# Two halves of the TensorE array: issue order of the forward transform's column products and second-pole products

## The chip, the cores and the metric

The kernel runs on one NeuronCore of a Trainium2 chip, as one launch. The metric is the device time of that launch in microseconds. The engines of the core are written as in the profile: PE (TensorE, matrix products), PEld (its weight loads), DVE (VectorE), ACT (ScalarE), POOL (GpSimd) and SP (which issues DMAs). All data are 32-bit floats.

## The reference

The input x has shape 16 x 16 x 256 x 256 (batch, channel, rows, columns). Two layers follow one another, and each is a group norm (8 groups of two channels) with a block behind it and the input added at the end. Layer 0 is a Laplace neural operator; layer 1 is a pair of small convolutions with an involution and a channel gate. The change is in layer 0:

```python
alpha = jnp.fft.fft2(x, axes=(-2, -1))
A  = 1.0 / (omega1[:, None, None, None] - weights_pole1[None])
Bm = 1.0 / (omega2[:, None, None, None] - weights_pole2[None])
S = jnp.einsum('ikpq,oikp,xikq->oxik', weights_residue, A, Bm)
output_residue1 = jnp.einsum('biox,oxik->bkox', alpha, S)
C = jnp.einsum('biox,oikp->bikpx', alpha, A)
D = jnp.einsum('bikpx,xikq->bikpq', C, Bm)
output_residue2 = jnp.einsum('bikpq,ikpq->bkpq', D, weights_residue)
```

`fft2` is done as two rounds of matrix products (first along rows, then along columns), and the projections on the poles, `C` and `D`, are matrix products as well.

## The kernel before

`forward` calls four stages one after another: `layer0_forward` (forward transform and pole projections), `layer0_mix` (channel mixing in frequency), `layer0_back` (inverse transform and second group norm) and `layer1`. The change is inside `layer0_forward` alone.

**The 64 steps.** A step handles one batch element `b` and one group `cg` of four channels. In step i PE works, in this order:

- `gn_mean` (L34): the group mean for the next step, and in the middle of the rows `gn_var` (L42). Between the two DVE computes `gnq` (L36 to L39) from the mean, so `gn_var` waits for DVE.
- `rows` (called twice, for two channels each): per channel eight products of 128 x 128 by 128 columns, alternately `pu` (L207, the row transform) and `pv` (L214, the first poles). ACT copies half of `pu` (`right`, L222), DVE adds and subtracts the halves into the spectrum tile `u` (L224), and ACT scales `pv` into `vt` (L231).
- `poles` (L241): the second poles, `pd`, for four channels.
- `columns` (L313): the column transform of the batch element before, out of `u`. Each call takes up to four of the 33 groups of frequencies. Steps with `cg` 0, 1 and 2 make two calls; a step with `cg` 3 makes three, the last for the single 33rd group. ACT moves `px` to `o` (L320), and POOL starts the DMAs that store `o` (L329).

The first four steps have no `columns`; after the last step all nine calls for the last batch element stand back to back. From step 4 on, one piece of the generator `tables` (the tables for the later stages, mostly DVE work, L400 to L530, and 16 small matrix products, L437) is put in per step until it runs out. PE's order is the order of the code (`manual_schedule` for PE); the order of the other engines is made by the scheduler. In `columns` the accumulator `px` has two buffers, and `o` has two.

**Halves of the array.** A product whose stationary operand has only 64 columns occupies half of the 128 columns of the array. Its output lands in PSUM partitions 0 to 63 or 64 to 127, according to the half. In `poles`, `a` selects the half (`pd[64 * a : ...]`); in `columns`, `k` does (`ps[64 * k : ...]`). A product of 32-bit floats is two instructions in the trace, so each call of `matmul` makes two weight loads and two MATMUL records. A chain of four products for one half is therefore eight records.

A product of the same shape as that in `columns`, 128 x 64 by 256 columns, stands in the next stage (`residues`, L635), and there the half is the innermost loop.

Of the kernel before, what the change touches and what calls it, by code (L numbers as in the profile page):

```python
# [72 lines left out]
def layer0_forward(ctx, tc, d, al, bd, tabs):  # L73
# [160 lines left out]
    def poles(cg, vts, acc):  # L234

        pd = psd.tile([P, 2, P], F32, tag="pd", name="pd")
        for j, vt in enumerate(vts):
            for a in range(2):
                ch = 4 * cg + 2 * j + a
                for n, (xh, k) in enumerate(((0, 0), (0, 1), (1, 0), (1, 1))):  # L240
                    nc.tensor.matmul(  # L241
                        pd[64 * a : 64 * a + 64, j],
                        lhsT=vt[:, a, xh, 64 * k : 64 * k + 64],
                        rhs=bt[:, xh, ch, 1 - k : 3 - k].rearrange("p l m -> p (l m)"),
                        start=n == 0,
                        stop=n == 3,
                    )
        gs = slice(2 * cg, 2 * cg + 2)

        def times(out, part, coef):  # L250
            shape = [P, 2, part.shape[2] // M, M]
            nc.vector.tensor_tensor(
                out.rearrange("p g (k q) -> p g k q", q=M),
                part.rearrange("p g (k q) -> p g k q", q=M),
                coef[:, gs].unsqueeze(2).to_broadcast(shape),
                ALU.mult,
            )

        t = dp.tile([P, 2, P], F32, tag="t", name="t")
        first = acc if cg == 0 else dp.tile([P, 2, P], F32, tag="t1", name="t1")  # L260
        times(first, pd, cr)
        times(t[:, :, :64], pd[:, :, 64:], ci)
        times(t[:, :, 64:], pd[:, :, :64], ci)
        if cg:
            nc.gpsimd.tensor_tensor(acc, acc, first, ALU.add)
        nc.gpsimd.tensor_tensor(acc[:, :, :64], acc[:, :, :64], t[:, :, :64], ALU.subtract)
        nc.gpsimd.tensor_tensor(acc[:, :, 64:], acc[:, :, 64:], t[:, :, 64:], ALU.add)
# [34 lines left out]
    def columns(b, g0, rsc):  # L302

        u = us[b % 2]
        n = min(4, NF - g0)
        o = op.tile([P, 2, 2, N], F32, tag="o", name="o")
        for j in range(0, n, 2):
            lanes = 64 * min(2, n - j)
            ps = psx.tile([P, 2, 2, H], F32, tag="px", name="px")
            for k in range(min(2, n - j)):  # L310
                for h in range(2):
                    for part in range(2):
                        nc.tensor.matmul(  # L313
                            ps[64 * k : 64 * k + 64, :, h],
                            lhsT=u[:, h, part, g0 + j + k].rearrange("p f c -> p (f c)"),
                            rhs=wxn[:, h, part],
                            start=part == 0,
                            stop=part == 1,
                        )
            nc.scalar.activation(  # L320
                o[:lanes, j // 2],
                ps[:lanes].rearrange("p v h x -> p v (h x)"),
                AF.Copy,
                scale=rsc[:lanes],
            )
        for k in range(min(2, n)):
            w = (n - k + 1) // 2
            for v in range(2):
                nc.gpsimd.dma_start(  # L329
                    out=al[g0 + k : g0 + n : 2, v, :, b].rearrange("g p x -> p g x"),  # L330
                    in_=o[64 * k : 64 * k + 64, :w, v],
                )
# [3 lines left out]
    with tc.manual_schedule(engines={mybir.EngineType.PE}):  # L336
# [6 lines left out]
        for i, (b, cg) in enumerate(steps):  # L343
            now, following = ready, iter(())
            if i + 1 < len(steps):
                following = halves(*steps[i + 1], *fetched.pop(0))
                next(following)
            v0 = rows(b, cg, 0, *now)
            next(following, None)
            if b and cg == 0:  # L350
                rsc = finish(b - 1, acc)
            v1 = rows(b, cg, 1, *now)
            ready = next(following, None)
            if cg == 0:
                acc = dp.tile([P, 2, P], F32, tag="acc", name="acc")
            if i == 0:
                table("2", *table_inputs("2"))
                passing.close()
            poles(cg, (v0, v1), acc)
            if b:  # L360
                for g0 in range(8 * cg, 8 * cg + 8 if cg < 3 else NF, 4):
                    columns(b - 1, g0, rsc)
            if i + 2 < len(steps):
                fetched.append(fetch(*steps[i + 2]))
            if i >= 4:
                next(pieces, None)
# [3 lines left out]
        for g0 in range(0, NF, 4):  # L370
            columns(nb - 1, g0, rsc)
# [1061 lines left out]
```

## Time and profile before

| | |
|---|---|
| device time, median of 3 | 7627.89 us (7627.58 to 7629.81) |
| span of the profiled execution | 7634.0 us |
| PE busy | 7110.6 us, 93% |
| DVE busy | 4906.0 us, 64% |
| ACT busy | 3674.3 us, 48% |
| POOL busy | 2832.8 us, 37% |
| `layer0_forward` | about the first 1420 us of the span |

A row of the table of groups reads: source line, engine, operation, output and inputs, the size of the array that is used (128*64 is 128 rows by 64 columns), shape of the moving operand, number of records, then busy time in us and mean duration of one record in ns, then idle time before it and what ended that. Durations of matrix products overlap because they are pipelined: 385 ns is the duration of one record, and the busy time is that of the union of all.

### The profile page before, as it was taken

To read this page: it belongs to the slowest core of one execution; us is meant where nothing else is said; L and a number is where in the kernel's file an instruction comes from. 1 tells how busy PE (TensorE), PEld (TensorE's weight loads), DVE (VectorE), ACT (ScalarE), POOL (GpSimd) and SP (SyncE) were. 2 spreads that over 40 slices of the span, in tenths; PEclk is the share of its full clock that TensorE was granted. 3 is DMA by queue.
4 is the path that set the end of the run, shared out by engine and by line. 5 is a ranking of instruction groups with operands and counts; after the bars stand their busy time and mean duration, and the time that the engine had idled before them with its cause. 6 is when DMAs were issued, how large, how long until landed. Compare 5 with 4: busy or idle time off the path is not lost. (4 is left out here: it accounts for less than half of the span.)

```text
span 7634.0 us, 147451 instructions
## 1 busy us (share of the span) xinstructions
PE 7110.6 (93%) x58728; PEld 4078.3 (53%) x58728; DVE 4906.0 (64%) x9184; ACT 3674.3 (48%) x5387; POOL 2832.8 (37%) x3616
## 2 busy tenths in 40 slices
PE   7889999799999998999979999999999999999997
PEld 5778888566666666777723333333333333333332
DVE  8999875366666665666656666666666666666662
ACT  2223333366666663111146655665665666565662
POOL 2334444211111111111145545555545555545552
PEclk9999999899999999999989999999999999999998
DMA  3344444333333335877757888899888898888886
GB/s 97 113 116 125 113 119 109 113 96 95 97 95 100 97 98 161 259 245 248 232 151 219 233 241 249 244 267 258 247 246 248 245 267 259 251 242 246 246 267 204
DMA packets 936290, 1442.20 MB, mean 189 GB/s; under 512 B 91866, under 2 KB 807958, under 8 KB 903606
## 3 DMA queue, kind: packets, MB, share of 16 engines
q1 hardware_dynamic: 792374, 958.51, 44.5%
q0 software_dynamic: 143232, 474.25, 19.7%
q8 instruction: 469, 7.68, 0.4%
q14 instruction: 215, 1.76, 0.1%
HBM read 875.87 MB, written 556.47 MB: 188 GB/s over the span
## 5 line engine op out<-in xcount | busy, mean ns | idle before, releaser
L1021 ACT ACTIVATE wide<-c,b 32x512 f32<-32x512 f32 x2176 | 1479.5, 680 | 371.9 <-PE c L972 319.7
L1049 DVE TENSOR_TENSOR t<-pd,r 64x512 f32<-64x512 f32 x1088 | 744.1, 684 | 1324.0 <-PE pd L1041 1301.0
L1052 DVE TENSOR_TENSOR top<-pd,t 32x512 f32<-32x512 f32 x2176 | 1503.1, 691 | 54.2 <-DMA cf<-top 1.4
L1115 PE MATMUL c2ps<-rows,c 128*32 128x512 f32 x12288 | 1392.4, 600 | 22.5 <-ACT e L1124 13.8
L972 PE MATMUL c<-z,w 102*128 102x512 f32 x2048 | 1052.2, 645 | 140.5 <-ACT wide L1021 117.1
L1033 POOL COPY wide<-wide 32x1031 f32<-32x1031 f32 (+1 forms) x576 | 569.0, 988 | 1392.7 <-ACT wide L1021 1365.4
L1041 PE MATMUL pd<-wide,dw 128*128 128x512 f32 x2048 | 1014.2, 617 | 5.9 <-ACT r L1009 3.5
L1115 PEld LDWEIGHTS c2ps<-rows,c 128*32 128x32 f32 x12288 | 388.0, 109 | 994.0 <-issue 889.4
L972 PEld LDWEIGHTS c<-z,w 102*128 102x128 f32 x2048 | 398.7, 197 | 703.4 <-issue 514.1
L1041 PEld LDWEIGHTS pd<-wide,dw 128*128 128x128 f32 x2048 | 377.2, 194 | 626.7 <-issue 456.7
L709 POOL DMA_DIRECT2D hd<-h x254 | 188.6, 742 | 1281.9 <-DVE h L705 1262.0
L1124 ACT ACTIVATE e<-c2ps,b 128x512 f32<-128x512 f32 x256 | 176.0, 687 | 857.5 <-PE c2ps L1115 854.8
L1034 POOL COPY wide<-wide 32x1031 f32<-32x1031 f32 (+1 forms) x576 | 572.3, 994 | 35.8
L313 PE MATMUL px<-wxn,u 128*64 128x256 f32 x4224 | 558.9, 385 | 2.6 <-ACT o L320 2.3
L839 PE MATMUL py<-h,iy 128*128 128x256 f32 x2048 | 541.6, 383 | 5.2 <-issue 5.2
L635 PE MATMUL ps<-tt,lt 128*64 128x256 f32 x4224 | 497.0, 385 | 37.8 <-DVE lt L621 34.0
L692 PE MATMUL ph<-ix,yt 64*128 64x256 f32 x4128 | 503.5, 391 | 7.4 <-issue 6.8
L313 PEld LDWEIGHTS px<-wxn,u 128*64 128x64 f32 x4224 | 401.0, 136 | 128.2 <-ACT o L320 5.7
L692 PEld LDWEIGHTS ph<-ix,yt 64*128 64x128 f32 x4128 | 393.6, 190 | 93.9 <-issue 46.5
L839 PEld LDWEIGHTS py<-h,iy 128*128 128x128 f32 x2048 | 385.2, 191 | 108.4 <-issue 50.0
L207 PE MATMUL pu<-fy,eo 128*128 128x128 f32 x2048 | 424.7, 291 | 12.0 <-DVE u L224 8.3
L594 DVE TENSOR_SCALAR alb<-alc,m 128x1024 f32<-128x1024 f32 x330 | 418.9, 1394 | 0.0
(202 smaller groups left out, 10008.6 us busy)
## 6 DMA issues: line engine op xcount, KB each, us to landing
rows<-cf SPq DMA_DIRECT2D x128, 2176.0 KB
z<-zn SPq DMA_DIRECT2D x768, 256.0 KB
cf<-top POOLq DMA_DIRECT2D x512, 240.0 KB, 7.3
cf<-bot POOLq DMA_DIRECT2D x96, 840.0 KB, 10.7
alc<-al SPq DMA_DIRECT2D x264, 256.0 KB
zn<-zb SPq DMA_DIRECT2D x128, 516.0 KB
o<-zn SPq DMA_DIRECT2D x64, 1032.0 KB
z<-in_x SPq DMA_DIRECT2D x64, 1024.0 KB
```

What stands on the lines that cost most here:

```text
L313: nc.tensor.matmul(ps[64 * k : 64 * k + 64, :, h], lhsT=u[:, h, part, g0 + j + k].rearrange("p f c -> p (f c)"), rhs=wxn[:, h, part], star ...
L635: nc.tensor.matmul(ps[64 * h : 64 * h + 64, v], lhsT=lt[:, h, k, 1 - v : 3 - v].rearrange("p l f c -> p (l f c)"), rhs=tt[:, h, k], start= ...
L692: nc.tensor.matmul(ph[q][:, e], lhsT=yt[lanes, i].rearrange("p t k -> p (t k)"), rhs=ix[lanes, i], start=n == 0, stop=n == 3,)
L839: nc.tensor.matmul(py[:, yh], lhsT=iy[:, v, ys], rhs=h[:, k, v], start=v == 0, stop=False)
L972: nc.tensor.matmul(ps[:, q], lhsT=w, rhs=cols[:, 1 - q], start=True, stop=True)
L1021: nc.scalar.activation(self.feat[64 - 32 * q : 96 - 32 * q, f, self.groups[g], :H], ps[32 * f : 32 * f + 32, q], AF.Mish, bias=b1[0][32 * ...
L1033: nc.gpsimd.tensor_copy(flat[0:32, f, 1:m], flat[64:96, f, 0 : m - 1])
L1034: nc.gpsimd.tensor_copy(flat[96:128, f, 0 : m - 1], flat[32:64, f, 1:m])
L1041: nc.tensor.matmul(ps, lhsT=dwt if self.tail else dw, rhs=self.feat[:, f, cs, :H], start=True, stop=True,)
L1049: nc.vector.tensor_tensor(t[64:128], ps[:64], self.r[:, cs], ALU.mult)
L1052: nc.vector.tensor_tensor(self.top[32 * f : 32 * f + 32, cs, q], ps[lanes], t[lanes], ALU.add)
L1115: nc.tensor.matmul(ps[32 * j : 32 * j + 32], lhsT=c2[:, blk, dx, :], rhs=t[:, 4 * j + blk : 4 * j + blk + 4, x : x + H], start=(blk, dx) = ...
```

## The change

The loops over the half move inward. In `poles` the four products of a chain are now the outer loop and the half `a` the inner one, and in `columns` the half `k` goes inside `h` and `part`. The products, their operands, their accumulation per half and their number stay the same: 2112 products in `columns` and 1024 in `poles`. Consecutive products now go to different halves of the array, so that two of them can run side by side. Building both programs shows the same order of instructions on DVE, ACT, POOL and SP.

```diff
         for j, vt in enumerate(vts):
-            for a in range(2):
-                ch = 4 * cg + 2 * j + a
-                for n, (xh, k) in enumerate(((0, 0), (0, 1), (1, 0), (1, 1))):
+            for n, (xh, k) in enumerate(((0, 0), (0, 1), (1, 0), (1, 1))):
+                for a in range(2):
+                    ch = 4 * cg + 2 * j + a
                     nc.tensor.matmul(
                         pd[64 * a : 64 * a + 64, j],
...
             ps = psx.tile([P, 2, 2, H], F32, tag="px", name="px")
-            for k in range(min(2, n - j)):
-                for h in range(2):
-                    for part in range(2):
+            for h in range(2):
+                for part in range(2):
+                    for k in range(min(2, n - j)):
                         nc.tensor.matmul(
                             ps[64 * k : 64 * k + 64, :, h],
```

## The prediction

> **What bounds the kernel now.** I read the groups of PE first, then busy time by stage, then PE's timeline in one step, then who waits for whom. All edits are in `layer0_forward`, so only its stretch of the span matters. The groups show the row to be changed and a twin that already alternates the halves:
>
> ```profile
> L313 PE MATMUL px<-wxn,u 128*64 128x256 f32 x4224 | 558.9, 385 | 2.6 <-ACT o L320 2.3
> L635 PE MATMUL ps<-tt,lt 128*64 128x256 f32 x4224 | 497.0, 385 | 37.8 <-DVE lt L621 34.0 <-issue 3.8
> L241 PE MATMUL pd<-bt,v 128*64 128x128 f32 x2048 | 164.6, 279 | 0.0
> ```
>
> The first two have the same shape, the same 4224 records and the same 385 ns each, yet the union is 558.9 us against 497.0. So the gain to be had is of the order of 62 us, and not the half of 559. The timeline of one step and of one burst of the twin say why:
>
> ```profile
> 1019.62 2.24 PE L241 MATMUL pd<-bt,v 128*64 128x128 f32 x29
> 1021.59 0.43 PE L313 MATMUL px<-wxn,u 128*64 128x256 f32 x1
> 1021.70 0.38 PE L241 MATMUL pd<-bt,v 128*64 128x128 f32 x2
> 1021.86 0.38 PE L313 MATMUL px<-wxn,u 128*64 128x256 f32 x1
> 1021.91 0.27 PE L241 MATMUL pd<-bt,v 128*64 128x128 f32 x1
> 1022.08 7.90 PE L313 MATMUL px<-wxn,u 128*64 128x256 f32 x62
> 1029.90 0.38 PE L34 MATMUL gn_mean<-mv,ones 128*128 128x2 f32 x2
> ```
> ```profile
> 1607.23 3.67 PE L635 MATMUL ps<-tt,lt 128*64 128x256 f32 x32
> ```
>
> The first `px` starts at 1021.59, before the last three `pd`, although it stands behind them in the program: PE already lets the next chain, which is for the other half, start before the chain ahead has ended. Record by record, starts in the middle of `px` follow 216, 6, 210, 57, 159, 57, 159, 57 ns, again and again: eight records (one chain) in 920 ns, or 115 ns each. One half alone would need 8 x 216 = 1726. In the twin the starts go 209, 7, 209, 7: two records in 215.8 ns, 108 each. What order costs today is mainly at the ends of a run: the first chain goes half alone, and the last four records go alone at 216 each.
>
> Next, the stages of the forward transform (columns: length, then busy us and records of PE, PEld, DVE, ACT, POOL, then clock, DMA share, GB/s):
>
> ```profile
> 166.40:552.20 385.80, 336.81 (x2662) 294.14 (x2661) 354.45 (x1047) 105.00 (x194) 137.84 (x189) 0.92 0.40 114
> 552.20:1019.60 467.40, 456.20 (x4065) 391.96 (x4064) 426.07 (x1085) 178.49 (x311) 219.65 (x300) 1.00 0.44 119
> 1019.60:1369.10 349.50, 349.50 (x3194) 304.36 (x3193) 187.30 (x568) 107.45 (x213) 166.05 (x234) 1.00 0.40 107
> ```
>
> Three regimes: steps 5 to 19, with table pieces, where DVE is busy 92%; steps 20 to 43, where PE is at 98% and DVE at 91%; and steps 44 to 62, where PE is busy for all of 349.50 us. The waits agree. The first line below is PE's in 166 to 545 us, the others are DVE's in 552 to 1019 us:
>
> ```profile
> PE gn_var L42 <- DVE gnq L39: 45.1, 15, 6.0
> ```
> ```profile
> DVE gnq L36 <- PE gn_mean L34: 10.8, 9, 2.0
> DVE arg L525 <- ACT n L523: 8.4, 10, 1.6
> DVE arg L515 <- DMA ed<-arg: 8.0, 6, 2.2
> DVE st L174 <- DMA z<-in_x: 7.6, 6, 2.5
> DVE u L224 <- ACT right L222: 1.1, 3, 0.6
> ```
>
> In the first regime PE waits for DVE in every step. In the second DVE waits for PE only 12 us in all.
>
> **What the Trainium skill says.** "TensorE: Matmul & The Clock Gate", Part 3, says that products in different column groups run side by side; the twin's 108 ns per record, half of the 216 that a lone half shows, agrees. The same part calls the order of matmuls strictly first in, first out, with only weight loads pulled ahead. The trace contradicts that for two halves (the `px` at 1021.59), and I take the trace: it is why the gain is small. Its Part 1 says that PE falls to half clock after an idle window of some 3.4 us. In steps 6 to 19 some 15 to 29 of the 64 row records start at 210 ns or so in place of 112, each time behind a gap of 2.0 to 6.2 us between two starts, so shorter idles suffice here.
>
> **The change part by part.** Nothing is added or removed, and no other engine's order moves. Only starts on PE change.
>
> *poles, per step.* Now 32 records from 1019.62 to the first `px` at 1021.59: 1.97 us. Alternating, they are 16 pairs. The middle of the present run, where both halves work, shows a pair in 109 ns, and the first record shows its weight load as 160 in place of 109. So 0.160 + 15 x 0.109 = 1.80 us: 0.18 saved.
>
> *columns, a step with two calls (64 records).* From the first `px` to `gn_mean` now 1029.90 - 1021.59 = 8.31 us. Alternating: 32 pairs at the twin's 215.8 ns. The last pair starts 31 x 0.2158 = 6.69 us after the first, and `gn_mean` follows the last start by 0.309 as today: 7.00 us. Saved: 1.31. Together 1.49 us per step.
>
> *columns, a step with cg 3 (72 records).* The 33rd group has only one half. Today it costs 0.92 us more (the run is 9.47 against 8.55 us to the first row product), because it runs beside the chain ahead. With all pairs full, its eight records are alone: 8 x 0.2158 = 1.73. So 0.81 of the 1.49 goes back: 0.68 saved.
>
> *Sum by regime.* Steps 44 to 62 are 15 of the first kind and 4 of the second: 15 x 1.49 + 4 x 0.68 = 25.1 us, all on the path. No other engine stops it: a step of 18.07 us becomes 16.58, where DVE has some 10 us of work, POOL 8.7, ACT 5.3. The waits of DVE for the input z there are for a step three ahead.
>
> Steps 20 to 43 would save 18 x 1.49 + 6 x 0.68 = 30.9 on PE, which takes PE's own 443.5 us (18 steps of 18.07 and 6 of 19.70) to 412.6. Counting each step by itself, DVE is busy 420 us in them, so DVE becomes the bound. What can go is what DVE waits for PE: 10.8 + 1.1 = 12 us; and part of the 8.4 for ACT's sine, which stands behind `o` in ACT's order, and `o` waits for `px`. I take 15 us. The DMA waits stay.
>
> Steps 5 to 19: `gn_var` waits for DVE in each, 2.0 to 6.2 us. An earlier end of `columns` makes this wait longer by the same amount. I take 0; a longer idle could keep PE cold for a few records more (-3), and the waits of DVE for `right` could shrink (+8).
>
> Steps 0 to 4: about 2 us (step 4 is bound by PE, the first four have `poles` alone). After step 63, nine calls stand back to back, 264 records in 33.9 us, 4.1 us a call, already above PE's 3.68 because `o` waits for its stores (ACT `o` on DMA, up to 2.3 us); PE's faster 3.45 brings little. With step 63 itself, 2 us.
>
> Sum: 25.1 + 15 + 0 + 2 + 2 = 44 us. 7627.9 - 44 = 7584.
>
> **The rivals.** *Second regime gains next to nothing:* DVE keeps its pace and PE goes cold in the gaps that open. For it: idles of 0.8 to 2.2 us before `gn_var` already stand in steps 21, 24, 32, 36 and 40, and 1.5 more brings them to the length that turned the clock down earlier. Against it: DVE's wait for `gn_mean` is real. Then 25 + 3 + 2 + 2 = 32: 7596.
>
> *Everything on PE's side pays:* the second regime saves its 31 and the first 8. For it: PE is at 98% in the second. Against it: DVE's 420 us. Then 25 + 31 + 8 + 4 = 68: 7560.
>
> *No change:* PE's own look-ahead already overlaps all that can be overlapped. Against it: the twin's 62 us. 7628.
>
> *Slower:* if alternation left each weight load open, a pair would take 216 + 51 (the 430 ns of the first record of a chain against 379) = 267 ns, and in `poles` 160: 31 x 0.267 + 0.309 = 8.59 us, 0.28 more than the 8.31 of today, and 16 x 0.160 - 1.97 = 0.59 more, together 0.87 a step. Over the 43 steps from 20 on that is 37 us, less where DVE hides it, say 25: 7653. Against it: the twin shows 260 once per burst and then 209.
>
> **How the numbers follow.** The forecast (a gain of 36 to 55) gets 0.55, the poor second regime 0.22, all of PE's side 0.13, no change 0.06, slower 0.04. The first three are faster by over 15 us: 0.90. The range reaches from a little beyond the large gain, 7558, to a little beyond the poor one, 7606, which leaves out no change and slower (0.10) and a tail of the rest.
>
> **What would show it right or wrong.** Starts in L313 alternating 209 and 7; its union near 495 to 505; a step in the third regime of 16.6 us, 19.0 with cg 3; the second regime near 452 us with DVE the busier engine; the first unchanged near 386, with a longer `gn_var` wait. A step in the third regime that stays at 18.07 would overturn the mechanism; one of 17 us or more would mean a cost of the alternation that the twin does not have.

## The result and the profile after

The changed kernel takes 7596.51 us (median; 7592.94 to 7610.79) against 7628.85 us: a ratio of 0.9961, 95% interval 0.9943 to 0.9978. So it is faster by 32 us. The forecast was 44 us faster (7584), and the rival in which steps 20 to 43 gain next to nothing named 7596.

The groups of PE after, in the same columns as before:

```profile
L635 PE MATMUL ps<-tt,lt 128*64 128x256 f32 x4224 | 495.8, 384 | 40.8 <-DVE lt L621 37.6 <-issue 2.0 <-ACT y L664 1.0
L313 PE MATMUL px<-wxn,u 128*64 128x256 f32 x4224 | 485.6, 381 | 11.0 <-ACT o L320 11.0
L241 PE MATMUL pd<-bt,v 128*64 128x128 f32 x2048 | 130.8, 279 | 0.1
```

L313 lost 73 us of busy time and now stands beside its twin L635; L241 lost 34. The two times overlapped before, so they can't be added, and the row products took 7 us more: PE's busy time as a whole fell by 70 us (7110.6 to 7040.6), and the kernel gained 32. Beside the new L313 stands an idle of 11.0 us before it, for ACT's `o`, where it was 2.6.

PE's timeline in one step of the last stretch (start, length, group) shows the order that was wanted: no product of the columns among those of the poles, and all 64 records in one run of 7.08 us.

```profile
1118.84 2.03 PE L241 MATMUL pd<-bt,v 128*64 128x128 f32 x32
1120.71 7.08 PE L313 MATMUL px<-wxn,u 128*64 128x256 f32 x64
1127.71 0.38 PE L34 MATMUL gn_mean<-mv,ones 128*128 128x2 f32 x2
```

From the first record to the group mean it is 7.00 us, as forecast, where it was 8.31. The stages by the same cuts as before (steps 5 to 19, 20 to 43, 44 to 62; length, then busy us and records of PE, PEld, DVE, ACT, POOL, then clock, DMA share, GB/s) say where the gain stayed:

```profile
164.20:551.90 387.70, 321.57 (x2664) 270.46 (x2662) 354.00 (x1047) 104.76 (x194) 137.75 (x189) 0.90 0.40 113
551.90:1016.40 464.50, 430.26 (x4065) 352.51 (x4064) 420.21 (x1086) 177.53 (x311) 220.41 (x300) 0.98 0.45 121
1016.40:1342.30 325.90, 325.90 (x3195) 270.61 (x3194) 187.26 (x568) 107.36 (x213) 166.21 (x234) 1.00 0.42 114
```

Set beside the lengths of before (385.80, 467.40, 349.50): +1.9, -2.9 and -23.6 us. In the middle stretch PE is busy 26 us less and the stretch is 3 us shorter: the rest became idle time of PE. PE's two longest waits there (us in total, times, longest), first before, then after:

```profile
PE pu L207 <- DVE u L224: 5.8, 5, 1.9
PE px L313 <- ACT o L320: 2.3, 2, 1.3
```
```profile
PE pu L207 <- DVE u L224: 19.3, 12, 2.3
PE px L313 <- ACT o L320: 10.3, 8, 2.3
```

PE stands still at a row product until DVE has emptied its accumulator `pu` into `u`, and at a column product until ACT has emptied `px` into `o`. For the variance it waits 0.8 us in all. DVE's waits in that stretch, after:

```profile
DVE arg L515 <- DMA ed<-arg: 11.4, 8, 3.0
DVE st L174 <- DMA z<-in_x: 9.0, 7, 2.4
DVE arg L525 <- ACT n L523: 8.4, 10, 1.7
DVE gnq L36 <- PE gn_mean L34: 5.9, 6, 1.6
DVE u L224 <- ACT right L222: 3.9, 5, 1.4
```

They sum to 38.6 us, where those of before summed to 35.9. The wait for the mean has fallen by 4.9 us, and waits for transfers and for ACT have grown by 7.6. DVE's busy time and these waits together make up 458.8 of the 464.5 us (462.0 of 467.4 before), so DVE has little free time in either kernel. Its busy time fell by 5.9 us with no work taken out. In both kernels some DVE instructions take over 0.4 us longer than the median of their kind, each of them while POOL subtracts (L194). This is such a pair in step 40, after:

```profile
937.74 2.36 POOL L194 TENSOR_TENSOR eo<-z 128x1024 f32<-128x1024 f32 x1 [2.05 <-PE pv L214]
937.77 2.34 DVE L51 TENSOR_TENSOR gnt<-gnt,gnv 128x2 f32<-128x2 f32 x1
```

The DVE instruction usually takes 0.16 us. Before, 19 instructions of the stretch were held up so, for 35.6 us in all; after, 16, for 29.2 us. So the 3 us that the stretch gained are no shorter waits: these grew by 2.7 us, and DVE was held up by POOL for 6 us less.

Step 40 shows how the waits moved. Before, from the mean on (L37 and L38, which follow L36 at once, are left out; the last line is PE's first row product after the variance):

```profile
952.97 0.16 DVE L36 TENSOR_TENSOR gnq<-mv,gn_mean 128x2 f32<-128x2 f32 x1 [1.97 <-PE gn_mean L34]
954.79 0.35 DVE L515 TENSOR_SCALAR arg<-etr,epi 128x256 f32<-128x256 f32 x1 [1.48 <-DMA ed<-arg]
955.06 0.15 DVE L39 TENSOR_TENSOR gnq<-gnq,mv 128x2 f32<-128x2 f32 x1
957.94 0.46 PE L207 MATMUL pu<-fy,eo 128*128 128x128 f32 x2 [1.22 <-DVE u L224]
```

And the same place after:

```profile
946.87 0.16 DVE L36 TENSOR_TENSOR gnq<-mv,gn_mean 128x2 f32<-128x2 f32 x1 [0.56 <-PE gn_mean L34]
949.64 0.39 DVE L515 TENSOR_SCALAR arg<-etr,epi 128x256 f32<-128x256 f32 x1 [2.41 <-DMA ed<-arg]
949.95 0.14 DVE L39 TENSOR_TENSOR gnq<-gnq,mv 128x2 f32<-128x2 f32 x1
952.82 0.46 PE L207 MATMUL pu<-fy,eo 128*128 128x128 f32 x2 [2.18 <-DVE u L224]
```

The mean comes earlier, and DVE's wait for it shrinks from 1.97 to 0.56. But L515, behind L38 in DVE's order, waits for the store of an earlier table piece, which ends 3.3 us after its issue (3.8 before): 1.48 becomes 2.41. The two waits together fell by 0.48 us, and the step by 0.44 (19.42 to 18.98), where PE had 1.41 less to do. Behind that store stand `gnq` (L39) and, after four more instructions without a gap, `u` (L224). PE gets `gnq` in time for its variance, but its next row product waits for that `u`: 2.18 us in place of 1.22.

### The profile page after: what moved, and what is told of

It is laid out like the page before. It is cut to its first block, busy times and chain, and to the rows that moved or that the text cites. A ratio compares the mean times of both kernels' runs of the same rounds, so it can differ in the third digit from the quotient of the medians.

```text
span 7609.0 us, 147451 instructions
## 1 busy us (share of the span) xinstructions
PE 7040.6 (93%) x58728; PEld 3973.2 (52%) x58728; DVE 4899.7 (64%) x9184; ACT 3670.0 (48%) x5387; POOL 2833.6 (37%) x3616
## 5 line engine op out<-in xcount | busy, mean ns | idle before, releaser
L635 PE MATMUL ps<-tt,lt 128*64 128x256 f32 x4224 | 495.8, 384 | 40.8 <-DVE lt L621 37.6
L313 PE MATMUL px<-wxn,u 128*64 128x256 f32 x4224 | 485.6, 381 | 11.0 <-ACT o L320 11.0
L214 PE MATMUL pv<-at,eo 128*128 128x128 f32 x2048 | 415.3, 286 | 0.0
```

The costliest lines, as they stand in the source:

```text
L313: nc.tensor.matmul(ps[64 * k : 64 * k + 64, :, h], lhsT=u[:, h, part, g0 + j + k].rearrange("p f c -> p (f c)"), rhs=wxn[:, h, part], star ...
L635: nc.tensor.matmul(ps[64 * h : 64 * h + 64, v], lhsT=lt[:, h, k, 1 - v : 3 - v].rearrange("p l f c -> p (l f c)"), rhs=tt[:, h, k], start= ...
```

## The experiments

The two theories after the result. *Pace:* DVE's amount of work on the table pieces, in its fixed order, sets the time of steps 5 to 43, so PE's saving turns into waiting there. *Clock:* PE has the saving but loses it to half clock in the wider gaps around the variance. A third was kept open: the alternation itself costs something outside the last stretch.

The time of each stretch, from each kernel's trace (from the start of a step's first L241 product to that of the first step after the stretch, in us), and the median of the whole. A stretch is read from one execution; `changed` and `after_again` are the same kernel and differ by up to 1.9 us in a stretch. The runs were made on several chips, on which the kernel before took 7626 to 7632 us; each ratio below is to the kernel before on the same chip.

| kernel | steps 5-19 | 20-43 | 44-62 | whole |
|---|---|---|---|---|
| before | 385.7 | 467.5 | 349.5 | 7628.9 |
| changed | 387.6 | 464.6 | 325.8 | 7596.5 |
| after_again | 386.9 | 462.7 | 325.8 | 7591.0 |
| poles_only | 385.9 | 466.3 | 346.5 | 7624.6 |
| columns_only | 387.8 | 463.9 | 334.5 | 7606.7 |
| no_tables_before | 277.6 | 443.5 | 349.5 | 7494.1 |
| no_tables_after | 260.6 | 414.5 | 325.9 | 7424.2 |
| arg_two | 386.9 | 468.4 | 325.9 | 7599.1 |
| early_mean | 399.4 | 532.3 | 355.1 | 7708.4 |
| early_arg | 397.4 | 531.4 | 339.7 | 7687.1 |
| warm | 378.5 | 498.7 | 326.4 | 7637.7 |
| t_last_before | 325.8 | 490.4 | 395.5 | 7634.6 |
| t_last_after | 328.4 | 492.9 | 372.1 | 7613.5 |
| split_last | 383.9 | 454.3 | 322.6 | 7581.7 |

**Each half of the change alone.** `poles_only` has the first hunk of the diff, `columns_only` the second.

> The second poles alternate, the columns stay as before. If a pair of halves is all there is to it, poles take 1.87 us in place of 1.97 and the run of columns keeps its 8.31 us to the group mean, since its half-alone first chain and its lone last four records stay: a step of steps 44 to 62 goes from 18.07 to about 17.97 us, 2 us in all, 7627 us, not to be told from before by the clock. If the alternation of poles cost a weight load per record, poles would take 2.56 us and the kernel be some 10 us slower.

> The columns alternate, the second poles stay as before. A step of steps 44 to 62 should take 16.75 to 16.85 us (7.25 from the first column product to the first row product, poles 1.97), with the 33rd group 19.2, so some 22 us from those steps; the whole about 7600 us. If the gain came from poles, 18 us a step and 7625.

`poles_only`: ratio 0.9997 (0.9988 to 1.0005), the last stretch 3.0 us shorter. `columns_only`: 0.9969 (0.9957 to 0.9981), the last stretch 15.0 us shorter, a step 17.19 us and not 16.8. The two add up to 18.0, and together they bring 23.6. PE's timeline of `columns_only` shows where the difference lies:

```profile
1122.40 2.24 PE L241 MATMUL pd<-bt,v 128*64 128x128 f32 x29
1124.38 0.43 PE L313 MATMUL px<-wxn,u 128*64 128x256 f32 x1
1124.48 0.38 PE L241 MATMUL pd<-bt,v 128*64 128x128 f32 x2
1124.64 0.38 PE L313 MATMUL px<-wxn,u 128*64 128x256 f32 x1
1124.70 0.27 PE L241 MATMUL pd<-bt,v 128*64 128x128 f32 x1
```

The last chain of the poles still occupies one half when the first column products of the other half begin. One half gets ahead of the other, and their starts stay 52 and 164 ns apart to the end of the run, so the run has a lone start and a lone end: 7.67 us to the first row product in place of 7.25. The first stretch and the middle one move by 4 us at most.

**The table work taken out**, with the old and with the new order of halves. In both, the arithmetic of the tables is left out, with DVE's part also ACT's (the sine) and the sixteen products on PE, and one constant is stored in their place, so the later stages work on other numbers.

```diff
+    flat = cp.tile([P, 2, N], F32, name="flat")
+    nc.gpsimd.memset(flat, 0.01)
     for k in range(C):
...
-        nc.sync.dma_start(out=td[:, :, k], in_=t)
+        nc.sync.dma_start(out=td[:, :, k], in_=flat)
```

> Halves in the order of before; the arithmetic of the tables for the later stages is left out (their memory is filled with one constant, with the same number of stores), which takes DVE's extra work out of steps 4 to 46. Later stages do the same work on other numbers. If DVE paces steps 5 to 43, all steps from 5 on fall to about 18.07 us (19.7 with the 33rd group), so the forward transform ends some 95 us earlier: about 7535 us. If something else paces them (stores, the input, the clock), they stay between 19 and 25 us.

> The same with the halves in turn. If DVE's table work was what kept the change from paying in steps 5 to 43, the steps are now 16.66 us (19.09 with the 33rd group) from 5 to 62, and this run is below its partner with the old order by 44 x 1.41 + 14 x 0.61 = 71 us, about 7464 us, where with the tables the change brought 32. If the alternation itself has a cost outside steps 44 to 62, or the input, the stores or the half clock take the time, the two differ by 20 to 40 us only.

The change now brings 69.9 us (7494.11 to 7424.22): 17.0, 29.0 and 23.6 in the three stretches. The stages of `no_tables_after`, columns as above:

```profile
161.50:422.10 260.60, 259.76 (x2543) 215.55 (x2542) 151.79 (x470) 85.19 (x170) 134.98 (x189) 1.00 0.51 141
422.10:836.60 414.50, 414.50 (x4059) 344.07 (x4058) 243.23 (x750) 136.30 (x271) 214.89 (x300) 1.00 0.47 126
836.60:1162.40 325.80, 325.80 (x3193) 270.64 (x3192) 182.64 (x561) 107.22 (x213) 166.35 (x234) 1.00 0.43 113
```

PE is busy for all of the middle stretch, and 414.5 is what the step times of the last stretch give: 18 x 16.66 + 6 x 19.09 = 414.4. So the alternation has no cost of its own outside the last stretch, and neither the input nor the stores of `o` hold the steps at this pace. What took the gain away in steps 5 to 43 is the table work. The pair doesn't tell its parts from one another: DVE's arithmetic, ACT's sine and the stores that DVE waits for. Nor does it tell the clock from them, as the clock is 1.00 in all three stretches of both. With the old order the steps fell to the times expected, 18.07 and 19.70 us (11 x 18.07 + 4 x 19.70 = 277.6 in the first stretch). The 95 us named with them were added up wrong: it is 108.1 + 23.9 = 132 us in the two stretches, and the whole came to 7494 and not to 7535.

**One fixed wait taken out of DVE's order.** The tile `arg` of the table pieces gets a second buffer, with the halves in turn.

```diff
-            arg = tp.tile([P, 2, N], F32, tag="arg", name="arg")
+            arg = tp.tile([P, 2, N], F32, tag="arg", name="arg", bufs=2)
```

> The halves in turn, and a second buffer for the tile arg of the table pieces, so that DVE need not wait for the store of the piece before. In the changed kernel DVE waits 11.4 us for that store in steps 20 to 43. If those fixed waits in DVE's queue keep the gain away, steps 20 to 43 fall from 464.5 to about 453 to 457 us and the whole to about 7587. If the half clock takes the gain, nothing changes: 464 and 7596.

The wait for the store fell from 11.4 to 0.8 us, and the middle stretch got no shorter (468.4). Other waits of DVE took its place:

```profile
DVE u L224 <- ACT right L222: 11.0, 17, 1.6
DVE gnq L36 <- PE gn_mean L34: 8.0, 3, 4.9
```

PE's wait for `u` grew as well, from 19.3 to 26.8 us. So this store is one of several things that DVE runs up against, and not the one that decides.

**The mean before the columns.** PE issues the mean for the step after next ahead of `columns`; the fetch of that input moves with it. `early_arg` has the second buffer as well.

```diff
             poles(cg, (v0, v1), acc)
+            if i + 2 < len(steps):
+                fetched.append(fetch(*steps[i + 2]))
+            following = iter(())
+            if i + 2 < len(steps):
+                following = halves(*steps[i + 2], *fetched.pop(0))
+                next(following)
             if b:
                 for g0 in range(8 * cg, 8 * cg + 8 if cg < 3 else NF, 4):
                     columns(b - 1, g0, rsc)
```

> The halves in turn, and the group mean of the step after next is issued on PE before the columns and not after them, so that DVE has the whole run of columns to compute gnq and PE finds it ready at the variance. If what keeps the gain away is that PE and DVE wait for each other at this point in turn, steps 20 to 43 fall from 464.5 towards the 420 us that DVE has work for, say 440, and steps 5 to 19 from 388 to about 375: the whole about 7560. If DVE's amount of work alone sets the pace, steps 5 to 19 stay within 5 us of 388 and steps 20 to 43 above 455: 7590. If the half clock is the cause, the gaps vanish with the wait and it falls as in the first case, with no row products at 210 ns.

> Both edits: the early mean and the second buffer for arg. If they act on the same waits, no better than the better of the two; if they add, some 8 us below the early mean alone, near 7550.

Both are slower than the kernel before (1.0099, 1.0086 to 1.0113, and 1.0078, 1.0065 to 1.0090). In `early_mean` DVE waits in the middle stretch for the input, and no longer for the mean:

```profile
DVE st L174 <- DMA z<-in_x: 61.6, 23, 5.8
DVE u L224 <- ACT right L222: 20.5, 21, 1.8
```

The scheduler now puts the statistics of an input (L174) in DVE's order directly behind the instruction that frees that input's buffer (L191). DVE then stands still for the whole transfer, up to 5.8 us. The mutual wait at the mean was removed, and a longer one put in its place, so this kernel doesn't tell what the mutual wait costs.

**PE kept busy in the gap.** Ten products that nothing reads, before the variance, in steps 5 to 43.

```diff
             v0 = rows(b, cg, 0, *now)
+            if 5 <= i < 44:
+                warm = psd.tile([P, P], F32, tag="pd", name="warm")
+                for _ in range(10):
+                    nc.tensor.matmul(warm, lhsT=ones, rhs=ones, start=True, stop=True)
```

> The halves in turn, and in steps 5 to 43 ten products of 128 x 128 by 128 columns that nothing reads, placed on PE just before the variance (20 records of 112 ns, 2.24 us), where PE waits for DVE anyway. They keep PE's clock up. If the half clock takes the gain of steps 20 to 43, these steps fall by the 2 us of each cold step (four of 24) to about 456 us, less what the added products cost where PE did not wait; if DVE paces them, 464 to 480 us, and steps 5 to 19 within 5 us of 388, with fewer row products at 210 ns in both stretches.

The record of a row product usually starts 112 ns after the one before it. Counted here are slow starts, those 200 to 230 ns after it. In steps 5 to 19 they fell from 245 to 115, and the stretch from 387.6 to 378.5 us, though PE had 15 x 2.24 = 34 us more to do. So the half clock seems to cost some 9 us there; but the table work also shifted (1071 DVE instructions in that stretch in place of 1047), so the figure is not shown by itself. In steps 20 to 43 the slow starts fell only from 51 to 35, and the stretch rose by 34 us for 54 us of added products. There the run says little about the clock, but the counts do: before the change the stretch had 6 slow starts, after it 51. The 45 more, at about 0.1 us each, are under 5 us of PE's time, where 26 us of the gain are missing. So the clock takes a small part there, and not the most of it. PE isn't far from binding either: work added to PE is paid for, work taken away is not.

**The table pieces in another order.** The sixteen pieces with matrix products go to steps 47 to 62, the others to steps 4 to 30. No work is left out.

```diff
-            if i >= 4:
+            if 4 <= i < 31 or i >= 47:
                 next(pieces, None)
```

> The halves in turn, and the table pieces in another order: the two kinds without matrix products in steps 4 to 30, the sixteen of L400 to L446 (with 1.73 us of PE each) in steps 47 to 62, where DVE was busy 10 us of 16.66. No work is left out. If DVE's amount of work per step sets the pace, steps 5 to 19 fall from 388 to about 300 us (5.4 us of DVE work and 1.73 of PE less in each), steps 20 to 43 stay near 465 or fall, steps 44 to 62 rise from 326 to about 354: some 60 us less, about 7535 us. If DVE's stops for transfers and for ACT set it, steps 5 to 19 fall by less than 30 us and the whole stays above 7590.

> The same order of table pieces with the halves in the order of before. If the change pays where PE sets the pace and is given back where DVE does, this run is above its partner with the halves in turn by more than the 32 us that the change brought: 25 us in the steps from 44 on and some 20 from the steps before, so 40 to 55 us, 7580 us. If the change can only pay in steps 44 to 62, the two differ by 25 to 32.

The order was no gain: steps 5 to 19 fell to 328 us and not to 300, and the middle stretch rose to 493, where the trace has the table work of these steps packed into fewer of them (it ends in step 35), and steps 44 to 62 rose to 372. But the pair tells how the change pays: 21 us between them, of which 23.4 in steps 44 to 62 and -2.6 and -2.4 in the two others. That is below what either theory gave. The middle stretch falls in two: in steps 36 to 43, without table work, the halves in turn are 9.7 us faster, and in steps 20 to 35, with it, 12.1 us slower (342.6 to 354.7). There the slow starts rose from 63 to 172, worth 11 us of PE's time, so the clock can be the cause of that loss; no run tells it from the waits. Where the table work stands, nothing of the change comes through.

**A step further, and the changed kernel again.** `split_last` gives the 33rd group to both halves, each with half of the moving columns, and keeps fourteen products that nothing reads in steps 5 to 19.

```diff
+        if n == 1:
+            ps = psx.tile([P, 2, 2, H], F32, tag="px", name="px")
+            for h in range(2):
+                for part in range(2):
+                    for v in range(2):
+                        nc.tensor.matmul(
+                            ps[64 * v : 64 * v + 64, 0, h],
+                            lhsT=u[:, h, part, g0].rearrange("p f c -> p (f c)"),
+                            rhs=wxn[:, h, part, P * v : P * v + P],
...
```

> The halves in turn; the products of the 33rd group, alone in its half, are split over both halves by their 256 moving columns (16 records of 128 columns in place of 8 of 256); and in steps 5 to 19 alone fourteen products that nothing reads stand on PE before the variance (28 records, 3.1 us), where PE waits 3.3 to 6.3 us for DVE. If the lone chain and the half clock in steps 5 to 19 are what they seem, a step with the 33rd group takes 18.2 us in place of 19.09 in steps 44 to 59 (3.5 us in all) and steps 5 to 19 about 375 in place of 388: some 15 us below the changed kernel. If DVE's work alone paces steps 5 to 19, only the 3.5 us remain.

> The changed kernel once more, to be compared with the others on the same chip: a ratio of 0.996 to before, and in the trace again about 326 us for steps 44 to 62 and 460 to 470 for steps 20 to 43 and 385 to 390 for steps 5 to 19, if the three stretches are as the first trace shows them and not an accident of one execution.

`after_again`: 7590.96 us, ratio 0.9947 (0.9934 to 0.9961), with the same three stretches within 2 us. `split_last`: 7581.67 us, 0.9939 (0.9926 to 0.9951), 9 us below. A step with the 33rd group takes 18.25 us in place of 19.09, and the last stretch is 3.2 us shorter, as expected. Steps 5 to 19 gave only 3.1, where 12 were expected, and the middle stretch gave 8.3, where six steps with the 33rd group at 0.84 make 5.0 at most. The traces give a likely reason for both: 36 DVE instructions more stand in the first stretch (1083 in place of 1047) and 35 fewer in the middle one (1050 in place of 1085), so table work had moved from the one to the other.

## Why the prediction was right, and where its middle term was not

- *The mechanism and its size.* Right. Pairs start at 209 and 7 ns, a run of 64 records takes the 7.00 us forecast. The union of L313 is 485.6 us, below the 495 to 505 that were named after the twin's 497.0.
- *Steps 44 to 62.* Forecast 25.1 us, measured 23.6. A step takes 16.66 us and not 16.58: the poles take 1.87 and not 1.80. Their second pair of chains opens like the first, with starts 153 ns apart in place of 103; why it does so wasn't tried. The step with the 33rd group takes 19.09 us against 19.02.
- *Steps 20 to 43.* This term was mis-sized: forecast 15 us, measured 2.9 (and 4.8 in the second execution), and PE stayed the busier engine (430 us to DVE's 420). The step that failed is "What can go is what DVE waits for PE". It counted DVE's waits for PE as time that would vanish (and with them 1.1 us before `u` that are a wait for ACT). They fell by 4.9 us at the mean, and the waits next in DVE's order grew by more. The bound on DVE was put at its 420 us of work, when its order with all its waits was the bound: busy time and waits fill all but 6 us of the stretch. That the table work holds the time there is shown by the pair without it, where the same stretch gains 29.0. That the time of one wait goes to others is shown for the store of `arg` and only seen in the trace for the rest; that DVE's part of the table work, and not ACT's, is what holds it is argued from DVE's full time.
- *Where PE waits in it.* The idles of 0.8 to 2.2 us in steps 21, 24, 32, 36 and 40, which the prediction puts before `gn_var`, stand behind it in the trace of before: they are the five waits of a row product for `u`.
- *Steps 5 to 19.* Forecast 0, measured +1.9 and +1.2. PE's wait for DVE before the variance took up the saving, as said: it grew from 45.1 to 60.6 us.
- *The rest.* Steps 0 to 4: forecast 2, measured 1.7. Step 63 and the nine calls behind it: forecast 2, measured 3.6 (45.0 to 41.4 us). The five parts sum to 30 us, and the medians differ by 32; the stages behind, which the change doesn't touch, took 6225 and 6214 us in two executions of the changed kernel, so the 2 us are within what they vary.
- *The rivals.* The poor middle stretch came about, and the time of the whole is the one that was named for it, 7596. The range held it because it was drawn to take in that case as well as the forecast. Of its two reasons, DVE's pace is the one that the runs support; PE did go cold more often, as was feared, but for under 5 us. A cost of weight loads in each pair did not appear.

## What to carry to other kernels

When two engines are nearly equally busy in a stretch, don't count one's wait for the other as time to be won. Follow the waiting engine's order to its next wait, and ask whether that one ends earlier too; if it is a transfer or another engine's answer, the gain can stop there. And see in the trace at which instruction the other engine stands still, as it need not be the one that looks likely in the code. Before pairing products for two halves of the array, look at the record starts: PE may overlap them already, and then only the ends of the runs and the odd chain are left to win or to lose.

## What the runs showed of the hardware

- PE started products out of the program's order where they belong to different halves of the array: before the change, a column product began at 1021.59 us, ahead of three pole products that stand before it in the program. A chain of eight took 920 ns so, where the lone records at the end of a run stand 216 ns apart, which is 1728 for eight.
- A skew between the halves stayed: in `columns_only` the starts were 52 and 164 ns apart through a whole run.
- Half clock came behind gaps between two starts as short as 2.05 us (step 13 of the kernel before, followed by 14 slow starts), and did not come behind one of 3.29 us (step 13 of the changed kernel).
- DVE instructions that usually take 0.16 us took up to 2.34 us while POOL's subtraction (L194, 2.36 us) ran; instructions so held up stand 16 to 19 times in steps 20 to 43. What links the two wasn't tried. Without the table work there was no such case.
